# Graph and relational attention on one core: the graph projection from seven products of quarters, the last norm's statistics on ScalarE

## The chip, the cores and the metric

The kernel runs on one core of one Trainium2 chip. The metric is the device time of one execution in microseconds, median of several runs; smaller is better. A core has TensorE (PE in the profile; its weight loads are listed apart as PEld), VectorE (DVE), ScalarE (ACT), GpSimd (POOL), and SyncE (SP), which here only issues DMA transfers. Each engine works through its own queue in order; they wait for one another through semaphores.

## The reference

64 graphs of 256 nodes with 256 features pass through two layers, all in fp32.

```
def layer0(x, adj):                       # two graph attentions, then a feed-forward
    for W, a in ((W1, a1), (W2, a2)):
        Wh = h @ W
        e  = leaky_relu(Wh @ a[:F] + (Wh @ a[F:]).T, 0.2)
        h  = softmax(where(adj > 0, e, -9e15), axis=1) @ Wh
    h = norm(x + h) * g1 + b1
    return norm(h + relu(h @ wf1 + bf1) @ wf2 + bf2) * g2 + b2

def layer1(x, adj):                       # 8 heads, relations r by value of adj
    A = softmax(q k^T / sqrt(32))
    o = sum over r of (A * (adj == r)) @ v_r
    x = norm(x + o @ Wo + bo) * g1 + beta1
    return norm(x + gelu(x @ W1 + b1) @ W2 + b2) * g2 + beta2
```

`norm` subtracts the mean of a row and divides by the square root of its variance plus 1e-5.

## The kernel before

The 64 graphs are taken as 32 pairs, `g[0]` to `g[31]`. A pair is a tile of 128 partitions by four blocks of 256 features. The kernel is a pipeline of 32 turns, `turn(y_, x_, z)` with `y_ = u`, `x_ = u + 1`, `z = u + 2`: in one turn pair y_ passes through layer 1, pair x_ through layer 0's feed-forward, and pair z through layer 0's graph attentions. A prologue brings pairs 0 and 1 to that point. Thirty turns have a pair z. In them the order on TensorE, SyncE, VectorE and ScalarE is the order in which the program writes the instructions (a manual schedule); GpSimd is left to the scheduler. Where two turns meet, the scheduler may interleave the end of one with the start of the next.

What the steps of the text refer to:

- *Seven products.* Most large products are computed as a 2 by 2 block product with seven quarter products instead of eight (Strassen's scheme in Winograd's form). `Projections` (L1047) does this for queries, keys and values, `hidden_seven` (L909) for the hidden layers, with step names such as "7a" (product 7, half a), `HiddenOut` (L998) for their output layers. Sums of operand quarters are made by VectorE (`sums`, s1 to s4). Seven products share two or three PSUM banks: a later product accumulates onto the bank of an earlier one, after the earlier result has been read out (`taken` or `add`). In `HiddenOut` product 6 accumulates onto product 1, 7 onto 6, 4 onto 7, and 3 onto 5.
- *The projection* `projected` (L767) forms xp = x @ W for pair z, with four extra columns for the attention scores, so 260 columns: two matmuls and one ScalarE copy for each of four blocks. Its input xT is the transpose of x, which `early` (L1171) makes on VectorE from the tile `xq`. `load_x` (L429) fetches xq. Then `score_rows` (L778) spreads a column of xp over rows, `Softmax` (L786) has the steps `raw`, `leaky`, `exp`, `masks`, `shares` and `scaled`, and `first_sums` (L1203) multiplies the attention with xp into `hp`.
- *PSUM banks.* `bank` (L423) hands out six banks of the tag "g"; two more, "po" and "zo", hold the attention's sums. `scores(n)` takes four banks of "g" for its heads, and `exps` (L1123) on ScalarE reads them out.
- *The last norm.* The finished y of the turn before waits in `waiting`. `moments` (L860) takes its statistics by VectorE's batch-norm instructions, `norm` (L870) makes the factor rs on GpSimd, `offsets` (L883) the shift, `applied_norm` (L887) normalizes on ScalarE, `affine` (L898) multiplies by the gain and adds the bias on VectorE (`times`, `plus`), `stored` (L1242) sends it off.
- *Division.* `shares(b, parts)` of a turn turns the attention's row sums into reciprocals (part 0) and divides (part 1); `out_(b)` then runs the output projection `yop`.

Of the kernel before, what the change touches and what calls it, by code (L numbers as in the profile page):

```python
# [16 lines left out]
P = 128  # L17
# [368 lines left out]
def narrow_path(  # L386
# [93 lines left out]
    other = const.tile([P, NG], F32, name="other")  # L480

# [56 lines left out]
    def gat_weights():  # L538

        w1s = work.tile([P, KB, F], F32, tag="hT", name="gw1")  # L540
        nc.scalar.dma_start(w1s, g_W1.rearrange("(c p) f -> p c f", p=P))
        w2e = work.tile([P, KB, WX], F32, tag="wh", name="gw2e")
# [138 lines left out]
    w2s, w2m = seven_out(w2, "w2")  # L681

# [84 lines left out]
    def projected(u, hT, blocks, xp):  # L767
        if xp is None:
            xp = work.tile([P, T, WX], F32, tag="wh", name=f"xp{u}")
# [63 lines left out]
    def gat_first(u, s, xp, hp=None, blocks=range(T)):  # L833
        if hp is None:
            hp = work.tile([P, T, WX], F32, tag="wh", name=f"hp{u}")
# [34 lines left out]
    def norm(u, l, y, blocks=range(T), mv=None, rest=range(NB, T)):  # L870
# [10 lines left out]
        return blocks, mv, rs, nm  # L881

# [220 lines left out]

    isd = 1.0 / math.sqrt(DH)
# [115 lines left out]
    def out_pieces(u, y, h1):  # L1220

        if u == NG - 2:
            s = [io.tile([P, T, N], F32, tag="y", name=f"sq{u}", bufs=4),
                 work.tile([P, T, WX], F32, tag="wh", name=f"wq{u}")[:, :, :N]]
# [51 lines left out]
    def turn(y_, x_, z):  # L1276
# [49 lines left out]
        with order:  # L1326
            p.sums()
            if X:
# [15 lines left out]
            if z + 1 < NG:  # L1344
                load_x(z + 1)
            if waiting:
                w, wy = waiting[0]
                last = moments(w, 3, wy, range(NB))
            if X:
# [4 lines left out]
                moved(moves, 3)  # L1354
                times(X["y"], rg1)
# [5 lines left out]
                if waiting:  # L1361
                    last = norm(w, 3, wy, mv=last)
# [6 lines left out]
                if waiting:  # L1369
                    offsets(*last)  # L1370
# [6 lines left out]
                if waiting:  # L1377
                    applied_norm(wy, *last, [0, 1])
# [4 lines left out]
                if waiting:  # L1383
                    applied_norm(wy, *last, [2, 3])
# [4 lines left out]
                first("ra")  # L1389
                scores(3)  # L1390
# [3 lines left out]
                shares(0, [0])  # L1394
                if not y_:
# [6 lines left out]
                first("5b 4a 6b 3b")  # L1402
                masks(3, (0,))
                if Z:
                    project(z, range(0, 1))
                first("rb 7b")
                if Z:
                    project(z, range(1, 2))
                first("sb")
                masks(3, (2,))  # L1410
                totals(3)
                sums(2)
                sums(3)
                first("4b")
# [32 lines left out]
            if X:  # L1447
                out = HiddenOut(x_, 0, X["y"], X["h1"], wf2s, out_sums(x_, 0))
                if Z:
                    out.sums(1, 2)  # L1450
            if Z:
                shares(1)
# [9 lines left out]
            if Z:  # L1462
                project(z, range(T // 2, T))
            if Z:
# [7 lines left out]
            if Z:  # L1472
                first_scores(z)
# [5 lines left out]
            if Z:  # L1479
                out(1)  # L1480
# [4 lines left out]
                out.sums(4)  # L1485
# [33 lines left out]
            if waiting and Z:  # L1519
                affine(waiting[0][1], rg4, rb4)  # L1520
                stored(*waiting.pop(), slice(0, T))
            if z + 1 < NG:
                load_rows(z + 1)
# [5 lines left out]
            if Z:  # L1529
                first_sums(z, range(T // 2, T))  # L1530
            if X:
# [79 lines left out]
    waiting, late = [], []  # L1611

    with tc.manual_schedule(engines={getattr(mybir.EngineType, n) for n in
# [75 lines left out]
        load_x(2)  # L1689
# [25 lines left out]
        first_sums(1)  # L1715
        affine(a["y"], rg1, rb1)
# [20 lines left out]
        made(wvm, 4)  # L1737
        first(3)
# [73 lines left out]
```

## Time and profile before

| | |
|---|---|
| median of three runs | 2960.92 us (2951.9 to 2962.96) |
| the profiled execution's own time | 2953.9 us |
| span in its profile, first to last instruction | 2952.3 us |
| granted TensorE clock | 0.998 |
| busy: PE, DVE, ACT, POOL | 99%, 88%, 64%, 21% |
| L773, projection matmuls | 512 records, 128.0 us, mean 383 ns |
| L866 and L867, moments of all norms | 512 of 408 ns and 512 of 182 ns |
| L895, normalizing activation of 256 | 592 ns |
| L775, copy of 260 columns from PSUM | 371 ns |
| L1014, quarter sum of 128x1024 | about 1.22 to 1.28 us |

Mean durations of matmuls overlap one another, and so do those of the other engines a little; what a stream costs is read from the distance between starts. A turn takes 90 us: the same instruction returns after that time. In a row of the profile, the line number is that of the program, `out<-in` names tiles, then come the shape and the number of instructions; brackets give the idle time of the engine before it and what ended it.

### The profile page before, as it was taken

The numbers are of one execution on the slowest core, as the hardware profiler recorded it, in microseconds if no ns is written. First come the engines' busy times: TensorE is split into PE (matmuls) and PEld (weight loads), VectorE is DVE, ScalarE is ACT, GpSimd is POOL, SyncE is SP. The second block draws the span as 40 slices with busy tenths as digits, with TensorE's granted clock in tenths as the row PEclk, the third lists the DMA queues.
The fourth block names the chain that finished last, engine by engine and source line by source line (L and its number), as shares of the span: only waits on it lengthen the run. The fifth ranks groups of instructions, "written<-read, shape, count | busy, mean of one in ns | idle before, by whom it ended". The sixth has DMA issues, their size and how long they took to land.

```text
span 2952.3 us, 58648 instructions
## 1 busy us (share of the span) xinstructions
PE 2921.4 (99%) x22206; PEld 2501.8 (85%) x22206; DVE 2612.6 (88%) x5027; ACT 1898.3 (64%) x3982; POOL 629.3 (21%) x930
## 2 busy tenths in 40 slices
PE   8999999999999999999999999999999999999997
PEld 7788888888888888888888888888888888888876
DVE  5889899989989898999898998899998989988987
ACT  5566666676676666666766766766667667667652
POOL 4212221122121122221221211222212212112211
PEclk9999999999999999999999999999999999999999
DMA  5011111111111111111111111111111111111000
GB/s 152 12 31 32 38 32 34 24 40 32 37 29 23 38 32 39 32 32 24 39 32 37 31 28 31 35 37 34 30 23 40 32 37 32 29 30 33 18 8 16
DMA packets 408020, 99.27 MB, mean 34 GB/s; under 512 B 357834, under 2 KB 407220, under 8 KB 407732
## 3 DMA queue, kind: packets, MB, share of 16 engines
q1 hardware_dynamic: 406332, 94.13, 14.8%
q8 instruction: 178, 2.92, 0.4%
q0 software_dynamic: 1056, 1.05, 0.1%
q14 instruction: 110, 0.90, 0.1%
q10 hardware_dynamic: 344, 0.28, 0.0%
HBM read 56.78 MB, written 16.78 MB: 25 GB/s over the span
## 4 chain that ended last, share of the span: by engine, by line
PE 96%; DVE 2%; ACT 1%; issue 0%; POOL 0%; DMA 0%; POOLq 0%; DVEq 0%; ACTq 0%
PE yf L1028 26%; PE h1a L939 15%; PE h1b L939 11%; PE po L1144 8%; PE v L1095 6%; PE qk L1095 6%; PE sp L1116 4%; PE hpp L840 4%; PE xpp L773 4%; PE ygp L851 4%; PE yop L851 4%; PE zo L1147 2%; PE rows L782 1%; DMA first<-in_adj_dram 0%; DVE st L866 0%
## 5 line engine op out<-in xcount | busy, mean ns | idle before, releaser
L1125 ACT ACTIVATE e<-sp 128x512 f32<-128x512 f32 x512 | 270.9, 611 | 71.4 <-issue 42.8
L1129 DVE TENSOR_TENSOR ea<-e,aT 128x1024 f32<-128x1024 f32 x256 | 310.9, 1216 | 1.8 <-ACT e L1125 1.8
L895 ACT ACTIVATE y<-y,nm,rs 128x256 f32<-128x256 f32 x442 | 235.1, 592 | 63.7 <-DVE nm L885 62.9
L948 DVE TENSOR_TENSOR h<-h1a,h 128x512 f32<-128x512 f32 x293 | 197.3, 682 | 80.7 <-PE h1a L939 77.3
L951 ACT COPY h<-h1b 128x512 f32<-128x512 f32 x293 | 175.2, 599 | 124.8 <-PE h1b L939 123.2
L957 ACT ACTIVATE h<-h,cols 128x256 f32<-128x256 f32 x512 | 221.9, 502 | 36.2 <-DVE h L948 32.0
L735 POOL COPY hT<-yt 32x256 f32<-32x256 f32 x244 | 211.5, 867 | 143.3 <-DVE yt L718 128.6
L1082 ACT COPY qk<-qk 128x512 f32<-128x512 f32 x128 | 74.4, 581 | 238.9 <-PE qk L1095 238.1
L866 DVE BATCH_NORM_STATS2 st<-y 128x6 f32<-128x256 f32 x512 | 208.6, 408 | 5.6
L877 POOL TENSOR_SCALAR rs<-mv 128x4 f32<-128x4 f32 (+1 forms) x134 | 41.5, 309 | 806.8 <-DVE mv L867 445.8
L1036 DVE TENSOR_TENSOR y<-yf,y 128x256 f32<-128x256 f32 x448 | 185.5, 414 | 30.5 <-PE yf L1028 30.5
L957 ACT ACTIVATE h<-h1a,cols 128x256 f32<-128x256 f32 x256 | 102.7, 464 | 131.8 <-PE h1a L939 131.8
L1157 POOL TENSOR_TENSOR low<-low,rq 128x16 f32<-128x16 f32 x64 | 14.0, 219 | 811.9 <-DVE rq L1156 811.9
L907 DVE TENSOR_TENSOR y<-y,rb 128x1024 f32<-128x1024 f32 x126 | 163.6, 1298 | 2.2
L1134 DVE TENSOR_TENSOR es<-e 128x1024 f32<-128x1024 f32 x128 | 155.8, 1217 | 0.0
L904 DVE TENSOR_TENSOR y<-y,rg 128x1024 f32<-128x1024 f32 x126 | 153.5, 1218 | 0.1
L878 POOL TENSOR_TENSOR rs<-rs,mhalf 128x4 f32<-128x4 f32 (+1 forms) x134 | 139.9, 1044 | 8.3
L939 PE MATMUL h1a<-tt,wf 128*128 128x256 f32 x512 | 137.7, 392 | 1.5 <-DVE h L948 1.5
L1116 PE MATMUL sp<-qk 32*128 32x256 f32 x2048 | 138.3, 394 | 0.0
L1144 PE MATMUL po<-e,v 128*32 128x256 f32 x2048 | 135.5, 382 | 0.0
L1144 PE MATMUL po<-ea,v 128*32 128x256 f32 x2048 | 134.4, 379 | 0.0
L718 DVE STREAM_TRANSPOSE yt<-y 128x256 f32<-128x256 f32 x364 | 128.3, 407 | 0.8 <-ACT y L895 0.7
(285 smaller groups left out, 7733.7 us busy)
## 6 DMA issues: line engine op xcount, KB each, us to landing
hT<-yt SPq DMA_DIRECT2D x666, 32.0 KB, 1.8
y<-in_x_dram SPq DMA_DIRECT2D x32, 512.0 KB, 4.2
xq<-in_x_dram SPq DMA_DIRECT2D x240, 64.0 KB, 2.1
aq<-in_adj_dram SPq DMA_DIRECT2D x240, 64.0 KB, 2.3
out_dram<-y SPq DMA_DIRECT2D x30, 512.0 KB
wf<-in_L_gnn_w_ff_dram SPq DMA_DIRECT2D x2, 1024.0 KB, 8.6
w<-in_L_gnn_W_dram SPq DMA_DIRECT2D x2, 1024.0 KB
first<-in_adj_dram POOLq DMA_DIRECT2D x2, 512.0 KB, 9.8
```

The source lines that it names most:

```text
L735: nc.gpsimd.tensor_copy(to, at)
L851: nc.tensor.matmul(ps[:, i * F:(i + 1) * F], lhs(t, k), rhs(b, k), start=(k == 0), stop=(k == n - 1))
L866: nc.vector.bn_stats(st[:, t, :], y[:, t, :])
L895: mark["normed"] = nc.scalar.activation(y[:, t, :], y[:, t, :], AF.Identity, bias=nm[:, t:t + 1], scale=rs[:, t:t + 1])
L939: nc.tensor.matmul(ps[:, i * N:(i + 1) * N], w_[:, f * P:(f + 1) * P], m, start=first and i == 0, stop=True, skip_group_check=True)
L957: nc.scalar.activation(y, y if ps is None else ps[:, i * N:(i + 1) * N], func, bias=bi[:, f:f + 1])
L1028: nc.tensor.matmul(s.ps[n][:, i * F2:(i + 1) * F2], a[:, k, i * P:(i + 1) * P], w_[:, k, :], start=n in (1, 2, 5) and i == 0 and k == 0, s ...
L1095: nc.tensor.matmul(ps[:, i * N:(i + 1) * N], l, r, start=n in (1, 2, 5) and i == 0, stop=True, skip_group_check=True)
L1116: nc.tensor.matmul(ps[a][:, j * N:(j + 1) * N], k_[hp, m, j0:j0 + P], q[hp, m, b * N:(b + 1) * N], start=True, stop=True)
L1125: nc.scalar.activation(e[:, a, :], ps[a], AF.Exp, scale=isd)
L1129: nc.vector.tensor_tensor(ea[:, a:a + 2, :], e[:, a:a + 2, :], ab[:, None, :].to_broadcast([P, 2, NB * N]), ALU.mult)
L1144: nc.tensor.matmul(po[hp, m * N:(m + 1) * N], vs[:, hp], w[:, a, j * N:(j + 1) * N], start=(n == 0), stop=(n == len(terms) - 1))
```

## The change

1. The projection of pair z is made from seven products of quarters by a new class `Projection`, with `gwe` and three derived quarters as moving operand and quarters of xT as stationary operand. Each product is two matmuls of 130 columns. Sums of quarters of xT are made in place by VectorE, so a sum that overwrites a quarter comes after the product that reads it. ScalarE copies the results of products 2, 5, 3 and 4, VectorE adds those of 1, 6 and 7. The steps are spread through the turn, and some neighbours are moved: `out.sums(2)` later, `out.product(1)` ahead of the score rows.
2. xp takes the buffer of xq, and `hp` has one buffer. So the loads of the next xq come after `first_sums`.
3. The last norm: ScalarE sums the rows (`row_sums`) and then the squared deviations (`deviations`), GpSimd makes mean, factor and shift. The normalization runs after `first_sums`; the gain, the bias and the store run in the next turn (`done`), and the load of pair z's rows follows the store.
4. The prologue makes the derived weight quarters on GpSimd and loads x of pair 2 later.

The diff, cut to its core:

```diff
+    gwes, gwem = seven(gwe, "gwe")
...
-            xp = work.tile([P, T, WX], F32, tag="wh", name=f"xp{u}")
+            xp = io.tile([P, T, WX], F32, tag="xq", name=f"xp{u}", bufs=1)
...
+    def row_sums(sm, y, blocks):
+        for t in blocks:
+            nc.scalar.activation(y[:, t, :], y[:, t, :], AF.Identity, accum_out=sm[:, t, 0:1])
+
+    def deviations(u, sm, y):
...
+        nc.gpsimd.tensor_scalar(nm, sm[:, :, 0], -1.0 / F, 0.0, op0=ALU.mult, op1=ALU.add)
+        for t in range(T):
+            nc.scalar.activation(dump, y[:, t, :], AF.Square, bias=nm[:, t:t + 1], accum_out=sm[:, t, 1:2])
+        nc.gpsimd.tensor_scalar(rs, sm[:, :, 1], 1.0 / F, EPS, op0=ALU.mult, op1=ALU.add)
+        nc.gpsimd.tensor_tensor(rs, rs, mhalf, ALU.pow)
+        nc.gpsimd.tensor_add(high, high, sm[:, :, 0])
+        nc.gpsimd.tensor_tensor(nm, nm, rs, ALU.mult)
+        return range(T), sm, rs, nm
...
+    class Projection:
+        def __init__(s, u, hT):
+            s.u = u
+            s.xp = io.tile([P, T, WX], F32, tag="xq", name=f"xp{u}", bufs=1)
+            s.h = [[hT[k][:, b * N:(b + 1) * N] for b in range(G)] for k in range(KB)]
+
+        def sums(s, *which):
+            (h00, h01), (h10, h11) = s.h
+            for n in which:
+                o, x_, y_ = ((h00, h01, h00), (h00, h11, h00), (h01, h11, h01), (h10, h10, h00))[n]
+                nc.vector.tensor_tensor(o, x_, y_, ALU.subtract)
+
+        def product(s, n):
+            a11, a12, a22, s1, s2, s3, s4 = gwes
+            (h00, h01), (h10, h11) = s.h
+            w, m = {1: (a11, h00), 2: (a12, h10), 5: (s1, h00), 3: (s4, h11),
+                    6: (s2, h00), 7: (s3, h01), 4: (a22, h10)}[n]
+            if n == 1:
+                s.one = bank(f"xp1_{s.u}")
+            elif n == 2:
+                s.two = bank(f"xp2_{s.u}")
+            ps, c = (s.two if n in (2, 5, 3) else s.one), WX // 2
+            for i in range(NB):
+                nc.tensor.matmul(ps[:, i * c:(i + 1) * c], m[:, i * P:(i + 1) * P], w,
+                                 start=n in (1, 2, 5) and i == 0, stop=True, skip_group_check=True)
+
+        def taken(s, n):
...
+            if n in (2, 5, 3, 4):
+                nc.scalar.copy(y, ps)
+            else:
+                nc.vector.tensor_tensor(y, ps, y, ALU.add)
...
             p.sums()
+            if done:
+                times(done[0][1], rg4)
...
             p("v5")
-            if z + 1 < NG:
-                load_x(z + 1)
+            if done:
+                plus(done[0][1], rb4)
             if waiting:
                 w, wy = waiting[0]
-                last = moments(w, 3, wy, range(NB))
...
                 moved(moves, 3)
+                if waiting:
+                    row_sums(sm, wy, range(3))
+                if done:
+                    stored(*done.pop(), slice(0, T))
+                if Z and y_:
+                    load_rows(z)
                 times(X["y"], rg1)
...
-                if waiting:
-                    last = norm(w, 3, wy, mv=last)
...
                 first("ra")
+                if waiting:
+                    row_sums(sm, wy, range(3, T))
                 scores(3)
                 masks(2, (0,))
                 if Z:
                     early(z)
                 shares(0, [0])
+                if Z:
+                    xp = Projection(z, g[z]["xT"])
+                    g[z]["xp"] = xp.xp
+                    xp.product(1)
+                    xp.sums(0, 2)
...
                 first("7a sa 1b")
                 shares(0, [1])
                 masks(2, (2,))
                 totals(2)
-                first("5b 4a 6b 3b")
+                if Z:
+                    xp(2)
+                first("5b")
+                if Z:
+                    xp(5)
+                first("4a 6b 3b")
                 masks(3, (0,))
                 if Z:
-                    project(z, range(0, 1))
+                    xp(3)
                 first("rb 7b")
-                if Z:
-                    project(z, range(1, 2))
                 first("sb")
+                if waiting:
+                    last = deviations(w, sm, wy)
                 masks(3, (2,))
                 totals(3)
                 sums(2)
                 sums(3)
+                if Z:
+                    xp.taken(1)
+                    xp.sums(1, 3)
+                    xp.product(6)
                 first("4b")
...
-                    out.sums(1, 2)
...
-                shares(1)
+                out.sums(1)
+                shares(1, [0])
+                xp.taken(6)
+                shares(1, [1])
...
-                project(z, range(T // 2, T))
-            if Z:
+                xp(7)
                 early_adjacency(z)
...
             out_(1)
+                xp(4)
+                out.product(1)
                 first_scores(z)
...
-                out(1)
+                out.add(1)
                 Z["m"].scores(0)
                 Z["m"].scores(1)
                 Z["m"].exp(0)
                 Z["m"].exp(1)
-                out.sums(4)
+                out.sums(2, 4)
                 offsets(*n)
                 out(2)
...
-            if waiting and Z:
-                affine(waiting[0][1], rg4, rb4)
-                stored(*waiting.pop(), slice(0, T))
-            if z + 1 < NG:
-                load_rows(z + 1)
...
+            if z + 1 < NG:
+                load_x(z + 1)
+            if waiting:
+                applied_norm(wy, *last, range(T))
+                if Z:
+                    done.append(waiting.pop())
```

More of the change, by code (lines that the diff above doesn't have):

```diff
@@ L480, in narrow_path @@
     other = const.tile([P, NG], F32, name="other")
+    dump = const.tile([P, F], F32, name="dump")
     def weight(w, name):
@@ L541, in gat_weights @@
         nc.scalar.dma_start(w1s, g_W1.rearrange("(c p) f -> p c f", p=P))
-        w2e = work.tile([P, KB, WX], F32, tag="wh", name="gw2e")
+        w2e = work.tile([P, KB, WX], F32, tag="wh", name="gw2e", bufs=1)
         nc.sync.dma_start(w2e[:, :, :F], g_W2.rearrange("(c p) f -> p c f", p=P))
@@ L834, in gat_first @@
         if hp is None:
-            hp = work.tile([P, T, WX], F32, tag="wh", name=f"hp{u}")
+            hp = work.tile([P, T, WX], F32, tag="wh", name=f"hp{u}", bufs=1)
         for t in blocks:
@@ L881, in norm @@
         return blocks, mv, rs, nm
+    def row_sums(sm, y, blocks):
+        for t in blocks:
+            nc.scalar.activation(y[:, t, :], y[:, t, :], AF.Identity, accum_out=sm[:, t, 0:1])
+    def deviations(u, sm, y):
+        nm = work.tile([P, T], F32, tag="nm", name=f"nm{u}_3")
+        rs = work.tile([P, T], F32, tag="rs", name=f"rs{u}_3")
+        nc.gpsimd.tensor_scalar(nm, sm[:, :, 0], -1.0 / F, 0.0, op0=ALU.mult, op1=ALU.add)
[6 more added lines that the diff above has]
+        return range(T), sm, rs, nm
     def offsets(blocks, mv, rs, nm):
@@ L1102, in __call__ @@
                 s.step(n[0], int(n[1]))
+    class Projection:
[22 more added lines that the diff above has]
+        def taken(s, n):
+            b, o = {1: (0, 0), 2: (0, 0), 5: (1, 1), 6: (1, 0), 3: (1, 0), 7: (1, 1), 4: (0, 1)}[n]
+            c = WX // 2
+            y = s.xp[:, b * NB:(b + 1) * NB, o * c:(o + 1) * c]
+            ps = (s.two if n in (2, 5, 3) else s.one)[:, :WX].rearrange("p (i n) -> p i n", i=NB)
+            if n in (2, 5, 3, 4):
+                nc.scalar.copy(y, ps)
+            else:
+                nc.vector.tensor_tensor(y, ps, y, ALU.add)
+        def __call__(s, n):
+            s.product(n)
+            s.taken(n)
     isd = 1.0 / math.sqrt(DH)
@@ L1223, in out_pieces @@
             s = [io.tile([P, T, N], F32, tag="y", name=f"sq{u}", bufs=4),
-                 work.tile([P, T, WX], F32, tag="wh", name=f"wq{u}")[:, :, :N]]
+                 work.tile([P, T, WX], F32, tag="wh", name=f"wq{u}", bufs=1)[:, :, :N]]
             s += [io.tile([P, T, N], F32, tag=t, name=f"sq{u}_{t}", bufs=1) for t in ("xq", "aq")]
@@ L1343, in turn @@
             p("v5")
-            if z + 1 < NG:
-                load_x(z + 1)
+            if done:
+                plus(done[0][1], rb4)
             if waiting:
                 w, wy = waiting[0]
-                last = moments(w, 3, wy, range(NB))
+                sm = work.tile([P, T, 2], F32, tag="mv", name=f"mv{w}_3")
             if X:
@@ L1368, in turn @@
                 masks(0, (0,))
-                if waiting:
-                    offsets(*last)
                 first("1a")
@@ L1376, in turn @@
                 first("2b 3a")
-                if waiting:
-                    applied_norm(wy, *last, [0, 1])
                 masks(1, (0,))
@@ L1382, in turn @@
                 totals(1)
-                if waiting:
-                    applied_norm(wy, *last, [2, 3])
                 scores(2, ())
@@ L1462, in turn @@
             if Z:
-                project(z, range(T // 2, T))
-            if Z:
+                xp(7)
                 early_adjacency(z)
@@ L1609, in turn @@
             waiting.append((y_, y))
-    waiting, late = [], []
+    waiting, late, done = [], [], []
     with tc.manual_schedule(engines={getattr(mybir.EngineType, n) for n in
@@ L1688, in narrow_path @@
         a["hT"] = features("h1T0", ph, (nc.scalar.copy, nc.vector.tensor_copy))
-        load_x(2)
         load_rows(2)
@@ L1715, in narrow_path @@
         first_sums(1)
+        load_x(2)
         affine(a["y"], rg1, rb1)
@@ L1737, in narrow_path @@
         made(wvm, 4)
+        made(gwem, 4)
         first(3)
```

## The prediction

> **What bounds the kernel now.** I read the page first: busy shares, then the chain that ended last.
>
> ```profile
> span 2952.3 us, 58648 instructions
> ...
> PE 2921.4 (99%) x22206; PEld 2501.8 (85%) x22206; DVE 2612.6 (88%) x5027; ACT 1898.3 (64%) x3982; POOL 629.3 (21%) x930
> ...
> PE 96%; DVE 2%; ACT 1%; issue 0%; POOL 0%; DMA 0%; POOLq 0%; DVEq 0%; ACTq 0%
> ```
>
> TensorE sets the end. But a matmul that waits a little still looks busy, so I compared one steady turn with its own spacing. The turn from 1350.95 to 1440.95 us lasts 90.0 us; its groups at their undisturbed spacing sum to about 89. So nearly all of it is matmul streaming, and VectorE, at 88%, is second. The gain can only be columns taken off TensorE; the loss is any new wait on it. Spacing, from the timeline of all engines (start, duration, instruction):
>
> ```profile
> 1392.52 1.92 PE L773 MATMUL xpp<-gwe,xT 128*128 128x260 f32 x8
> ...
> 1394.28 1.89 PE L851 MATMUL yop<-wo,qk 128*128 128x256 f32 x8
> ...
> 1396.44 3.74 PE L1028 MATMUL yf<-wf,h 128*128 128x128 f32 x32
> ...
> 1400.01 3.74 PE L1028 MATMUL yf<-wf2t,eq 128*128 128x128 f32 x32
> ```
>
> One fp32 matmul shows as two records. Four projection matmuls of 260 columns take 1394.28 - 1392.52 = 1.76 us; 32 records of 128 columns take 3.57 us, 112 ns each.
>
> Where the new work begins (same view; brackets: idle time before and what ended it):
>
> ```profile
> 1375.30 1.24 DVE L1175 STREAM_TRANSPOSE xT<-xq 128x1024 f32<-128x1024 f32 x1
> ...
> 1376.30 1.15 PE L1116 MATMUL sp<-qk 32*128 32x256 f32 x16
> ...
> 1377.38 1.13 PE L939 MATMUL h1a<-tt,wf 128*128 128x256 f32 x4
> ...
> 1378.55 0.69 DVE L948 TENSOR_TENSOR h<-h1a,h 128x512 f32<-128x512 f32 x1 [1.10 <-PE h1a L939]
> ```
>
> ScalarE's first exponential of that score group, alone:
>
> ```profile
> 1377.52 0.60 ACT L1125 ACTIVATE e<-sp 128x512 f32<-128x512 f32 x1 [1.20 <-issue]
> ```
>
> And from the score rows of the next pair to the product that uses s4:
>
> ```profile
> 1396.00 0.60 PE L782 MATMUL rows<-ident,xp 128*128 128x128 f32 x4
> ...
> 1396.64 1.57 ACT L800 ACTIVATE s<-rows,xp 128x256 f32<-128x256 f32 x4 [1.79 <-PE rows L782]
> ...
> 1398.43 0.43 DVE L1036 TENSOR_TENSOR y<-yf,y 128x256 f32<-128x256 f32 x1 [0.33 <-PE yf L1028]
> ...
> 1398.77 1.28 DVE L808 SCALAR_TENSOR_TENSOR s<-s 128x512 f32<-128x512 f32 x2
> ...
> 1399.97 1.22 DVE L1014 TENSOR_TENSOR eaq<-h,eq 128x1024 f32<-128x1024 f32 x1
> ...
> 1402.20 0.42 DVE L1036 TENSOR_TENSOR y<-yf,y 128x256 f32<-128x256 f32 x1
> ...
> 1403.59 0.61 PE L1028 MATMUL yf<-wf,eaq 128*128 128x128 f32 x4
> ```
>
> The addition at 1402.20 releases the bank into which the product at 1403.59 accumulates: 1.0 us of slack today.
>
> **What the Trainium skill says.** "TensorE: Matmul & The Clock Gate", § Wait — 56ns, not 53.3ns?: a streamed matmul takes N/2.4 GHz plus about 2.5 ns. Two passes of 128 give 111.7 ns; the trace has 112. The same page, § Step-by-step, says that only weight loads are pulled ahead and matmuls stay in program order, so one that waits holds all behind it; the rows above start in program order. "PSUM — Partial Sum Buffer", § Terms: a bank must not be written by TensorE while another engine reads it. So a product into a bank not yet read out must wait; no run here could show the violation. "ScalarE: Activation LUTs", § What ACT_TABLE_LOAD costs: 186 ns + 0.833 ns per element, each pointer operand 93 more. For 256 elements with two pointers that is 585 ns; the normalization's row (L895) has 592.
>
> **The change, part by part, per turn (90 us, 30 turns with a third pair z).**
>
> *Columns.* Out: eight matmuls of 260 columns, 2 x 1.76 = 3.51 us. In: fourteen of 130, 28 records x 112 x 130/128 = 3.17 us (0.45 per product). **-0.34 us.**
>
> *ScalarE.* Four copies of 260 elements (371 ns) stay four. The normalization's four activations (2.08 us) move later. New: four row sums (skill's price 399 ns) and four squares (492), each with an accumulator read, 187 ns at L765. I take 0.6 each, bounds 0.4 and 0.8. Three row sums fall in the 1.73 us idle before the copy at 1362.38, the squares in the 4.00 us before 1391.00, the normalization in the 2.27 us before 1413.49. Cost 0. Without cover the three sums would delay the last projection copies by up to 2.4 us, and the exponentials behind them.
>
> *VectorE.* Out: four moment pairs, 2.1 us by spacing, and an offset. In: four differences of 256 (0.34 to 0.46 by spacing, 1.5 in all) and three additions from PSUM (0.34, as L1036; 1.0). The scale (1.22) runs at the turn's start, in the 1.25 us in which VectorE waits for POOL's rs; the shift takes the place of the first two moment pairs. So total work is +0.4 us, but its place counts: the 2.1 us leave a stretch before 1364.3, the 2.5 us land between 1377 and 1396, where VectorE had 1.4 us idle in 19.
>
> *POOL and SP.* POOL's three small norm operations become five, 20 us ahead of use: 0; the four weight sums in the prologue, some 3 us once, hidden between 0 and 3. On SP the store, then the load of rows into its buffer, wait for the shift and for the store's landing (2.4 us); nothing else is queued there until 1405. The eight x loads go behind the graph sums: issued in 4.8 us near 1411, ahead of the twelve moves at 1421, landing 50 us before use. 0; without that, moves late by the same 5 us would stop TensorE.
>
> *New waits on TensorE.*
> (1) Product 1 stands right after the last score group. Then all six banks of the pool are live: four of scores, two of hidden products. It must wait for the first exponential, 1377.52 + 0.60 = 1378.12, plus 0.1 for the semaphore. TensorE arrives at 1377.38: **+0.85**. In the kernel before, a product with its own bank stood here and covered this.
> (2) Product 5 takes product 2's bank after its copy, behind the delayed `sa`: **+0.1**.
> (3) VectorE goes on at 1378.87 instead of 1378.55. Until the second half of the divided outputs it has its 14.55 us, plus differences 1.5, plus additions 0.68, minus the quarter sum moved away 1.14, plus some 0.3 of waiting for matmuls: ready 1394.8. The second output product gets there at 1394.28 (0.45 of projection ahead of it, no longer 1.75): **+0.6**. Product 4 then waits for product 7's addition, behind the output addition and two moment pairs: **+0.3**.
> (4) From the rows to product 3: 0.64 until ScalarE starts, 0.95 until the first leaky step, 0.70 and 0.60 for the two, 1.26 and 1.14 for the sums 2 and 4 (2 is new here), 0.07, 0.34, 0.68 for offset, addition, masks, 0.42 for the addition that frees the bank, 0.1: 6.9 us. TensorE has 0.44 + 3 x 1.79 = 5.8 to cover it; before it had four products, 7.6, as product 1 stood behind the rows. **+1.05.**
> (5) Product 7 then waits for the difference s3: **+0.2**. The graph sums need the scaled xp at about the time at which TensorE comes: 0.
>
> Sum: -0.34 + 0.85 + 0.1 + 0.6 + 0.3 + 1.05 + 0.2 = +2.76 us; x 30 = 83 us. Upon the profiled execution's 2953.9 (span 2952.3): **3037 us**. That execution lies 7 below the median of the runs, 2960.9, within their spread (2951.9 to 2963.0). Each wait is bounded by 0 below, and by about 0.4 more than I took above.
>
> **Rivals.**
> *Only the fewer columns count:* ScalarE's exponentials come earlier, or a bank is free, and VectorE's new work fits its gaps. -0.34 x 30 = -10, at best another 0.25 per turn from gaps: 2936 to 2945. For it: VectorE waits 1.10 us at 1378.55, room for two differences, and ScalarE has room. Against: six live banks and the 5.8 to 6.9 do not hang on VectorE's load. It decides if both (1) and (4) are under 0.1. This is the rival on the other side.
> *Only part of the waits:* (4) alone gives (1.05 - 0.34) x 30 = +21, 2975; (1) and (4) give +47, 3001. For it: (3) and (5) rest on VectorE's spacing, summed over 16 us.
> *ScalarE binds too:* row sums at 0.8 and late normalization delay the hidden copies at 1413 by up to 1 us: 3067. Against: 64% busy.
>
> **How the numbers follow.** All waits 0.50 (3014 to 3060), part 0.24 (2970 to 3014), columns only 0.20 (2936 to 2965), more 0.06. A difference under 0.5%, 15 us, is about what cannot be told from no change. Columns only mostly falls inside that: faster 0.08, same 0.15, slower 0.77. Range 2948 to 3062: it leaves out most of the faster cases and the worst, some 0.15. The likeliest case's own is 3014 to 3060.
>
> **What would show it.** Projection groups of 130 columns spaced 0.45 us; the first of them 0.8 us after the scores, ended by ScalarE's exponential; a gap before the second `yop` group and before the s4 product; the turn at 92 to 93 us; VectorE idle 0.7 before the leaky step. A turn of 89.7 us would prove me wrong, and a first product right after the scores would refute (1).

## The result

The changed kernel took 3063.62 us in the median of six runs (3056.64 to 3067.74), the kernel before 2961.72 (2951.9 to 2963.05, six runs): a ratio of 1.0351, 95% interval 1.0335 to 1.0366. The prediction had the direction and most of the mechanism. Its point was 3037 us in a range of 2948 to 3062 us; the time lies 27 us above the point and 1.6 us beyond the upper end of the range. In the profiles of this case the first turn begins either about 90 us or about 98 us after the first instruction (89.8 us in the changed kernel, 97.8 us in a variant with the same source up to there), so single times can differ by 8 us for that reason alone, and gains are read below from the length of a turn.

### The profile page after: what moved, and what is told of

It is laid out like the page before. It is cut to its first block, busy times and chain, and to the rows that moved or that the text cites. A ratio compares the mean times of both kernels' runs of the same rounds, so it can differ in the third digit from the quotient of the medians.

```text
span 3054.9 us, 60089 instructions
## 1 busy us (share of the span) xinstructions
PE 2965.5 (97%) x22566; PEld 2503.9 (82%) x22566; DVE 2620.1 (86%) x4967; ACT 2011.9 (66%) x4462; POOL 607.5 (20%) x994
## 3 DMA queue, kind: packets, MB, share of 16 engines
q0 software_dynamic: 1056, 1.05, 0.2%
## 4 chain that ended last, share of the span: by engine, by line
PE 48%; DVE 29%; ACT 14%; issue 4%; POOL 3%; DMA 1%; DVEq 0%; ACTq 0%; SPq 0%; POOLq 0%
PE yf L1047 9%; PE h1b L958 8%; PE h1a L958 7%; PE po L1206 6%; DVE eq L1033 4%; ACT h L976 4%; PE hpp L842 4%; DVE y L923 3%; PE sp L1178 3%; PE v L1114 3%; PE xp L1149 3%; DVE eaq L1033 3%; PE qk L1114 2%; DVE st L868 2%; DVE y L1055 2%
## 5 line engine op out<-in xcount | busy, mean ns | idle before, releaser
L737 POOL COPY hT<-yt 32x256 f32<-32x256 f32 x244 | 176.1, 722 | 133.7 <-PE qk L1114 81.4
L879 POOL TENSOR_SCALAR rs<-mv 128x4 f32<-128x4 f32 (+1 forms) x104 | 26.2, 252 | 720.7 <-DVE mv L869 495.0
L868 DVE BATCH_NORM_STATS2 st<-y 128x6 f32<-128x256 f32 x392 | 161.0, 412 | 4.6
L923 DVE TENSOR_TENSOR y<-y,rg 128x1024 f32<-128x1024 f32 x126 | 160.0, 1270 | 0.1
L1047 PEld LDWEIGHTS yf<-wf,eaq 128*128 128x128 f32 x1024 | 119.1, 192 | 38.2 <-DVE y L1055 25.6
L1047 PE MATMUL yf<-wf,eaq 128*128 128x128 f32 x1024 | 130.9, 282 | 20.0 <-DVE y L1055 19.7
L1158 ACT COPY xp<-xp 128x260 f32<-128x260 f32 x120 | 44.4, 370 | 153.4 <-PE xp L1149 153.4
L976 ACT ACTIVATE h<-h1a,cols 128x256 f32<-128x256 f32 x256 | 102.6, 464 | 61.3 <-PE h1a L958 61.3
```

What stands on the lines that cost most here:

```text
L868: nc.vector.bn_stats(st[:, t, :], y[:, t, :])
L923: nc.vector.tensor_mul(y, y, g_[:, None, :].to_broadcast(list(y.shape)))
L976: nc.scalar.activation(y, y if ps is None else ps[:, i * N:(i + 1) * N], func, bias=bi[:, f:f + 1])
L1047: nc.tensor.matmul(s.ps[n][:, i * F2:(i + 1) * F2], a[:, k, i * P:(i + 1) * P], w_[:, k, :], start=n in (1, 2, 5) and i == 0 and k == 0, s ...
```

## The profile after

The page of the changed kernel, its profiled execution at 3056.64 us:

```profile
span 3054.9 us, 60089 instructions
...
PE 2965.5 (97%) x22566; PEld 2503.9 (82%) x22566; DVE 2620.1 (86%) x4967; ACT 2011.9 (66%) x4462; POOL 607.5 (20%) x994
...
PE 48%; DVE 29%; ACT 14%; issue 4%; POOL 3%; DMA 1%; DVEq 0%; ACTq 0%; SPq 0%; POOLq 0%
```

The shares of busy time hardly moved. The chain did: TensorE's part of it fell from 96% to 48%, and VectorE and ScalarE now release what TensorE waits for. TensorE is "busy" 44 us more, although it has fewer columns to stream, because a matmul that waits a little is drawn longer; so I count by distances between starts. A turn, taken at the first query product of two turns, is 93.42 us long, before 89.97. The 3.45 us, times 30 turns, are 103 us, and 101.9 were measured. In the two traces, 102.2 of the 102.6 us by which the span grew lie between the first query products of the first and of the thirty-first turn: the loss lies in the turns, not in the prologue.

Two sets of products meet in what follows: products 1, 2, 5, 3, 6, 7 and 4 of the projection (tile `xp`) and those of the feed-forward's output (tile `yf`). Products 1, 2, 4 and 5 are the projection's, and products 3, 6 and 7 the feed-forward's where nothing else is said.

TensorE in one turn of after, which starts at 1306.30 (timeline: start, duration, engine, line, operation; in brackets idle time and what ended it):

```profile
1314.43 1.13 PE L1114 MATMUL qk<-tq,wqk 128*128 128x256 f32 x4 [0.20 <-ACT qk L1101]
...
1332.29 1.15 PE L1178 MATMUL sp<-qk 32*128 32x256 f32 x16
1334.15 0.71 PE L1149 MATMUL xp<-gwe,xT 128*128 128x130 f32 x4 [0.71 <-ACT e L1187]
...
1336.43 0.61 PE L1149 MATMUL xp<-gwe,xT 128*128 128x130 f32 x4
1336.87 1.03 PE L958 MATMUL h1b<-tt,wf1s 128*128 128x256 f32 x4
...
1350.67 1.99 PE L853 MATMUL yop<-wo,qk 128*128 128x256 f32 x8 [0.21 <-DVE qk L1226]
1352.79 0.71 PE L1149 MATMUL xp<-gwe,xT 128*128 128x130 f32 x4
...
1357.35 4.01 PE L1047 MATMUL yf<-wf2t,eq 128*128 128x128 f32 x32
1361.99 2.05 PE L1047 MATMUL yf<-wf,eaq 128*128 128x128 f32 x16 [0.64 <-DVE y L1055]
```

A quarter product of the projection costs 0.44 to 0.45 (1336.43 to 1336.87), as forecast; over all turns it is 0.446, so that seven take 3.12 where the eight matmuls of 260 columns took 3.51: -0.39. The first one comes 1.86 us after the score group ahead of it, which itself needs 1.08: 0.78 of waiting for the first exponential. `yop` is 0.37 late (0.82 after the product ahead of it instead of 0.45), and takes 2.12 to the next start where it took 1.73 before, and product 4 takes 0.55 instead of 0.44: 0.50 more. The 32 records at 1357.35, products 5 and 6 of the feed-forward, need 3.58, and product 3 starts after 4.64: 1.06, of it 0.17 ahead of product 6 and the rest ahead of product 3. Around product 7, later in the trace, the distances are 1.89, 1.91 and 1.89 instead of 1.79, 1.74 and 1.79: 0.37. Ahead of product 7 itself the trace names the cause. Its weight load (PEld) waits for the quarter sum s3, which ends 0.05 before it:

```profile
1364.38 1.36 DVE L1033 TENSOR_TENSOR eaq<-h 128x1024 f32<-128x1024 f32 x1
...
1365.79 1.86 PEld L1047 LDWEIGHTS yf<-wf,eaq 128*128 128x128 f32 x16 [0.41 <-DVE eaq L1033]
```

All of these stand where the prediction put them. The first row of the turn does not: the product of quarters q7, at 8.13 us into the turn, waits for ScalarE's copy of q6. In the kernel before it starts 7.77 us into its turn, which begins at 1350.95, and without idle time:

```profile
1358.72 1.03 PE L1095 MATMUL qk<-tq,wqk 128*128 128x256 f32 x4
```

By the first score group 0.64 us are lost (12.82 us into the turn, before 12.18): 0.36 ahead of q7, 0.17 and 0.11 behind it. That loss is not in the prediction. I call it wait (0).

VectorE in the same trace, where the turn before ends:

```profile
1304.77 0.40 DVE L868 BATCH_NORM_STATS2 st<-y 128x6 f32<-128x256 f32 x1
1305.08 1.21 DVE L923 TENSOR_TENSOR y<-y,rg 128x1024 f32<-128x1024 f32 x1
1306.20 0.18 DVE L869 BATCH_NORM_AGGREGATE mv<-st 128x2 f32<-128x6 f32 x1
1306.29 0.66 DVE L856 TENSOR_TENSOR y<-ygp,y 128x512 f32<-128x512 f32 x1
...
1309.72 0.16 DVE L904 SCALAR_TENSOR_TENSOR nm<-mv,rs 128x4 f32<-128x4 f32 x1 [1.25 <-POOL rs L880]
```

And the same place in the kernel before, whose turn starts at 1350.95:

```profile
1350.20 0.66 DVE L854 TENSOR_TENSOR y<-ygp,y 128x512 f32<-128x512 f32 x1
...
1353.62 0.16 DVE L885 SCALAR_TENSOR_TENSOR nm<-mv,rs 128x4 f32<-128x4 f32 x1 [1.25 <-POOL rs L878]
```

The scale (L923), written at the start of the turn, behind its first sums, has run in the middle of the statistics that end the turn before. The output addition behind it starts at -0.01 us of the turn instead of -0.75, and the offsets at 3.42 instead of 2.67. The 1.25 us of idle time, in which the prediction put the scale, is still there. What hangs on the offsets is about as late: ScalarE's normalization, and behind it in ScalarE's queue the copies of q5, q6 and v6. The normalization and the copy of q6, after:

```profile
1309.92 2.08 ACT L914 ACTIVATE y<-y,nm,rs 128x256 f32<-128x256 f32 x4 [1.05 <-DVE nm L904]
...
1313.79 0.58 ACT L1101 COPY qk<-qk 128x512 f32<-128x512 f32 x1
```

And before:

```profile
1353.81 2.08 ACT L895 ACTIVATE y<-y,nm,rs 128x256 f32<-128x256 f32 x4 [0.29 <-DVE nm L885]
...
1357.77 0.59 ACT L1082 COPY qk<-qk 128x512 f32<-128x512 f32 x1
```

They start 3.62 and 7.49 us into the turn instead of 2.86 and 6.82.

VectorE between the score rows of the next pair and product 3, after:

```profile
1356.69 1.42 DVE L810 SCALAR_TENSOR_TENSOR s<-s 128x512 f32<-128x512 f32 x2 [0.72 <-ACT s L802]
1358.03 1.22 DVE L1033 TENSOR_TENSOR eq<-eq,h 128x1024 f32<-128x1024 f32 x1
1359.28 1.22 DVE L1033 TENSOR_TENSOR eaq<-h,eq 128x1024 f32<-128x1024 f32 x1
...
1361.52 0.42 DVE L1055 TENSOR_TENSOR y<-yf,y 128x256 f32<-128x256 f32 x1
```

Quarter sum 2 (1358.03) now stands between the leaky step and sum 4, with 0.72 us of idle time ahead of the leaky step, and the addition that frees product 3's bank ends at 1361.94, 0.05 before the product.

## The experiments

All of these kernels compute the whole reference. My theory was the list of waits with (0) added; the rival, that VectorE or ScalarE has simply too much to do, in which case a wait that is taken away comes back further on. A time without an interval is one execution, and its 8 us at the start can hide a gain; the length of the turn does not contain them.

### The scale behind the last addition of the turn

```diff
             p.sums()
-            if done:
-                times(done[0][1], rg4)
...
             out(4)
+            if done:
+                times(done[0][1], rg4)
             waiting.append((y_, y))
```

> The gain of the last norm (times(done), 1.22 us of VectorE) is written behind the last addition of a turn instead of behind p.sums() of the next one. Theory W (single waits, each with its place): it fills VectorE's 1.25 us wait for rs, the offsets come 0.75 us earlier, TensorE no longer waits for the copies of qk and v: the turn shrinks from 93.4 to 92.8 us, the profiled time from 3057 to about 3038. Rival A (ScalarE is late because of its new row sums): no change, 93.4.

Measured: turn 93.24, 3062.04 us. Forecast 92.8: missed, a gain of 0.18 only. The scale did go where it was meant to, behind the statistics. VectorE there:

```profile
1406.71 1.22 DVE L923 TENSOR_TENSOR y<-y,rg 128x1024 f32<-128x1024 f32 x1
1408.85 0.16 DVE L904 SCALAR_TENSOR_TENSOR nm<-mv,rs 128x4 f32<-128x4 f32 x1 [0.92 <-POOL rs L880]
```

GpSimd in the same run, the power that makes rs:

```profile
1406.96 1.85 POOL L880 TENSOR_TENSOR rs<-rs,mhalf 128x4 f32<-128x4 f32 x1
```

The same power takes 1.04 us in the kernel before and in after; beside the scale it takes 1.85, and ends 0.88 after the scale's end. So the idle time was not free: what VectorE runs in it puts off what it is waiting for, and 0.46 of the 0.64 us stay. The Trainium skill describes such a case ("SBUF — State Buffer", § Who interferes with whom): an instruction of VectorE with two inputs in SBUF contends with a GpSimd instruction that reads SBUF, for a read interface that only one of them holds at a time. The times agree with it: the power begins 0.25 after the scale, and 0.88 of it is left when the scale is over, though spans on GpSimd are rough. 29 powers of this run take 1.85, none in after.

### Product 1 behind step 7a

```diff
-                    xp.product(1)
-                    xp.sums(0, 2)
...
-                first("7a sa 1b")
+                first("7a")
+                if Z:
+                    xp.product(1)
+                    xp.sums(0, 2)
+                first("sa 1b")
```

> Product 1 of the projection stands behind hidden product 7a instead of right behind the last scores, with its two differences. Theory W: it no longer waits for the first exponential to free a bank (0.71 us of wait on record), and VectorE goes on about 0.7 us earlier, so that the wait of the second output product shrinks too: turn 92.3 to 92.7 us, about 3022 to 3036 us. Rival V (VectorE has too much work between 1332 and 1356, wherever it starts): the wait comes back at the second output product and product 4, turn 93.1 or more.

Measured: turn 92.55, 3040.55 us. The wait for the bank is gone and the turn is 0.87 shorter, its 0.78 and the 0.08 of product 5. A product that has its bank now covers the exponential. The waits at `yop` and behind it stayed as they were, although the forecast had that at `yop` shrinking.

### Sum 2 ahead of the leaky step

```diff
                 out.add(1)
+                out.sums(2)
                 Z["m"].scores(0)
...
-                out.sums(2, 4)
+                out.sums(4)
```

> The quarter sum s2 of the first feed-forward stands ahead of the leaky step, where VectorE waits 0.72 us for ScalarE, instead of behind it. Theory W: the chain from the score rows to product 3 loses 1.26 and gains about 0.45, and the wait ahead of product 3 (with that ahead of product 6 1.06 us) falls to 0.2 to 0.4: turn 92.6 to 92.8 us, about 3033 to 3039. Rival V: no gain, 93.3 or more, the graph sums wait instead.

Measured: turn 92.35, 3034.63 us, a gain of 1.06, more than the 0.6 to 0.8 that I gave it. TensorE there:

```profile
1351.72 3.74 PE L1047 MATMUL yf<-wf2t,eq 128*128 128x128 f32 x32
1355.31 2.05 PE L1047 MATMUL yf<-wf,eaq 128*128 128x128 f32 x16
```

3.59 us from one to the other instead of 4.64: the whole wait ahead of products 6 and 3 is gone. Sum 2 fits the idle time ahead of the leaky step, and a wait that I had put down to a chain of 6.9 us was an order in it.

### These three together

> The three moves together. Theory W: the waits are separate, so their gains add, -0.64 - 0.9 - 0.7: turn 91.1 to 91.4 us, time 2985 to 2997. Rival V: VectorE's work binds, the turn stays above 92.2, over 3020. If moving removed all waits the turn would be 89.7.

Measured: 2999.98 us (2995.58 to 3005.66), ratio 1.0149, interval 1.0124 to 1.0174; turn 91.30. The gains add: 0.18 + 0.87 + 1.06 = 2.11, and 93.42 - 91.30 = 2.12. The turn is as forecast, the time 3 us above the forecast's upper end. None of the waits had hidden another one.

### Each half of the change alone

The norm's half alone keeps parts 2 and 3 of the change, and takes the eight products back to their places:

```diff
-                    xp.product(1)
-                    xp.sums(0, 2)
...
-                first("4a 6b 3b")
+                first("5b 4a 6b 3b")
...
+                    project(z, range(0, 1))
...
+                    out.sums(1, 2)
...
-                xp(7)
+                project(z, range(T // 2, T))
...
-                out.sums(2, 4)
+                out.sums(4)
```

The projection's half alone takes the last norm back:

```diff
-                times(done[0][1], rg4)
...
-                plus(done[0][1], rb4)
...
-                sm = work.tile([P, T, 2], F32, tag="mv", name=f"mv{w}_3")
+                last = moments(w, 3, wy, range(NB))
...
-                    row_sums(sm, wy, range(3))
...
-                    last = deviations(w, sm, wy)
...
+                affine(waiting[0][1], rg4, rb4)
```

> Only the last norm's part of the change (statistics on ScalarE, scale and shift a turn later, loads and buffers as changed); the projection again from eight products, with the quarter sums and the first output product where they were before. Theory W: the four waits around the projection are gone, only that at the turn's start stays, turn 90.5 to 90.7 us, time 2972 to 2983. Rival A (ScalarE's extra work holds others): 91 or more, over 2990. If the norm's part cost nothing: 90.0, as before.

> Only the projection from seven products, with its loads, buffers and moved neighbours; the last norm as before (moments on VectorE, scale and shift in the middle of the turn). Theory W: the wait at the turn's start is gone, those at the bank, at the second output product and product 4, and at the s4 product stay or grow by the moments on VectorE, turn 92.7 to 93.2 us, 3035 to 3052. Rival: without VectorE's relief the turn is far longer than with it, 94 or more; that would say that the norm's part paid for itself.

Measured, norm alone: 2974.98 us (2971.42 to 2979.18), ratio 1.0054, interval 1.0035 to 1.0074; turn 90.60, and the only wait in it is (0), at 8.12 us into the turn. Projection alone: turn 92.76, 3049.81 us; q7 at 7.77 as before, and the waits for the bank (0.71 in brackets), at `yop` (0.21) and at product 3 (0.64) all as in after. Over the turn before they cost 0.63 and 2.79, together 3.42 of the 3.45. So wait (0) belongs to the norm alone, (1) to (5) to the projection alone, and neither half pays for the other. ScalarE's new sums cost nothing here: the norm's half has no loss beyond the 0.63 up to the first scores.

### Scale and shift together behind v5

```diff
             p.sums()
-            if done:
-                times(done[0][1], rg4)
...
             p("v5")
             if done:
-                plus(done[0][1], rb4)
+                affine(done[0][1], rg4, rb4)
```

> The gain of the last norm stands right ahead of its bias, behind the transposes and v5, and so neither ahead of the last statistics nor beside GpSimd's power for rs (which took 1.85 us instead of 1.04 in the run before with the gain beside it). Theory P (the gain is in the way of the norm's offsets, by its place): TensorE's wait of 0.64 us for the copies of qk and v goes, turn 92.7 to 92.9 us, about 3035 to 3042 us. Rival A (the row sums on ScalarE): still 93.2 to 93.4.

> Product 1 behind 7a, s2 ahead of the leaky step, gain and bias together behind v5. Theory W: against the three moves before (91.3 us with the gain at the turn's end) another 0.46 go, turn 90.8 to 90.9 us, 2979 to 2985; what is left is 0.76 at the second output product and product 4 and 0.36 at the graph sums, less the 0.34 of fewer columns. Rival V: VectorE's new work only moves the wait, 91.2 or more.

Measured, alone: turn 93.31, 3061.74 us; with the other moves: 3003.57 us (2998.27 to 3005.29), ratio 1.0150, interval 1.0131 to 1.0169, turn 91.36. Both forecasts missed. In the run alone q7 starts at 7.78 again, but the wait has moved three products on:

```profile
1323.56 1.13 PE L1114 MATMUL qk<-tq,wqk 128*128 128x256 f32 x4 [0.25 <-DVE qk L1098]
```

The two pieces, 2.5 us, now stand together ahead of VectorE's additions for the queries and values (L1098), and q4 is 0.42 late for them, the first scores 0.53. Here the rival of the second forecast holds (91.2 or more): the work only moves the wait. The number of the first one's rival, 93.2 to 93.4 with ScalarE's row sums as the cause, fits too; but q7 is on time with these sums in place, and the next run takes the rest away with them in place as well.

### The scale behind v5, the shift behind the first hidden step

```diff
-                plus(done[0][1], rb4)
+                times(done[0][1], rg4)
...
-                if done:
-                    stored(*done.pop(), slice(0, T))
-                if Z and y_:
-                    load_rows(z)
...
                 steps = first_hidden(x_)
+                if done:
+                    plus(done[0][1], rb4)
+                    stored(*done.pop(), slice(0, T))
+                if Z and y_:
+                    load_rows(z)
```

> The changed kernel with two pieces of the last norm moved: the scale (VectorE, 1.21 us) goes to where the shift stood, behind the copy of v5, and the shift with its store and the load of the next rows goes on past the first hidden step of the feed-forward. The scale alone then takes the 1.2 us that the shift took at that place, so the copy of q4 should not be late as it was with scale and shift together (10.78 us into the turn), and the offsets' steps start early enough for q6 and v6. Theory: wait (0) is gone and none comes in its place; the turn falls by 0.5 to 0.7 us from 93.42 to about 92.8, the time to about 3040 us. Rival: the 1.2 us of the shift are now late somewhere else on VectorE (the copies behind the first hidden step); then the turn stays at 93.2 or more.

Measured: turn 92.77, 3046.16 us: a gain of 0.65, the whole of wait (0), and q7, v7, q4 and the first scores stand at 7.77, 8.64, 10.36 and 12.18 us into the turn, as in the kernel before. A store and a load that start later cost nothing. The turn is that of the projection alone, 92.76: with the scale and the shift at these places the norm's half costs nothing. Wait (0) was one of place, not of VectorE's load.

### All moves, with the first sums of x ahead of 7a

To the last run, product 1 behind 7a and sum 2 ahead of the leaky step, this adds:

```diff
+    apart = const.tile([P, N], F32, name="apart")
...
-                o, x_, y_ = ((h00, h01, h00), (h00, h11, h00), (h01, h11, h01), (h10, h10, h00))[n]
+                o, x_, y_ = ((apart, h01, h00), (apart, h11, apart), (h01, h11, h01), (h10, h10, apart))[n]
...
-            w, m = {1: (a11, h00), 2: (a12, h10), 5: (s1, h00), 3: (s4, h11),
-                    6: (s2, h00), 7: (s3, h01), 4: (a22, h10)}[n]
+            w, m = {1: (a11, h00), 2: (a12, h10), 5: (s1, apart), 3: (s4, h11),
+                    6: (s2, apart), 7: (s3, h01), 4: (a22, h10)}[n]
```

so that sums 0 and 2 need not wait for product 1 and stay ahead of 7a.

> All of the waits that I found are taken on together: the scale and the shift as in the run with the shift later; the second sum of the output ahead of the leaky scores (as in the third run); product 1 of the projection behind step 7a; and the first difference of x in a tile of its own, so that its sums need not wait for the last read of the old one and run in VectorE's idle time of 1.1 us ahead of 7a, which would let the waits of the second output product (0.37) and of product 4 (0.39) go. Theory: each wait goes without a new one, and the turn is 91.36 (the four moves) less 0.53 (q4), 0.76 (output product and product 4) and up to 0.36 (around product 7), so 89.7 to 90.1 us, the time 2950 to 2965 us: level with the kernel before. Rival: VectorE has no idle time left ahead of these places (its load of 86% binds there), the waits of product 4 and of the output product stay, and the turn is 90.8 us or more, the time over 2985 us.

Measured: 2981.78 us (2980.86 to 2983.57), ratio 1.0084, interval 1.0067 to 1.0102; turn 90.83. The three gains add again (93.42 - 0.65 - 0.87 - 1.06 = 90.84), and the tile apart brought nothing: the rival's turn, though not its time of over 2985. In this trace VectorE is idle for only 0.12 us between 1395.97 and 1423.6, and the rest of the loss lies in that stretch: 0.37 at `yop`, 0.50 behind it, 0.37 around product 7. The next two runs ask whether order or load makes them.

### Only the order in that stretch

```diff
-                out.sums(1)
                 shares(1, [0])
                 xp.taken(6)
                 shares(1, [1])
+                out.sums(1)
...
+                xp(7)
                 mv = moments(y_, 2, y, range(NB))
...
-                xp(7)
                 early_adjacency(z)
```

> The last kernel with two pieces of VectorE's order in the output stage changed and nothing added or removed: the mask product of the feed-forward (1.22 us) goes behind the second normalised attention output, on which the second output product waits, and product 7 is taken up ahead of the norm's statistics, so that product 4 finds its tile free. In its trace VectorE has no idle time from 16 us before to the end of product 3 (1395.97 to 1425.0), so the two ideas of what the waits are part here. If each wait is due to the order alone, the waits of the output product (0.37) and of product 4 (0.39) go and the turn is 90.83 less 0.76, about 90.1. If VectorE's whole load in this stretch is what binds, both waits go from where they were and come back around product 7 and the second graph sums, and the turn stays at 90.7 to 90.9. I expect the second.

Measured: turn 90.72, 2978.55 us. `yop` and product 4 now start without a wait, and TensorE stands again ahead of product 3:

```profile
1418.13 2.05 PE L1048 MATMUL yf<-wf,eaq 128*128 128x128 f32 x16 [0.59 <-DVE y L1056]
```

The two waits were worth 0.87 here (0.37 and 0.50); 0.75 are lost at product 3, which starts 4.33 us after the 32 records ahead of it instead of 3.58. Product 3 starts 53.02 us into the turn, and 53.13 us into it in the run before: the same work of VectorE stands ahead of it, in another order. Here VectorE's load binds, and a better order only moves the wait. (The stretch without idle time that the forecast names ends at 1423.66 in that trace, not at 1425.0; product 3 lies within both.)

### Less work in that stretch, in the old order

```diff
+            s.free = s.xp[:, :NB, WX // 2:WX // 2 + P]
...
-                o, x_, y_ = ((apart, h01, h00), (apart, h11, apart), (h01, h11, h01), (h10, h10, apart))[n]
+                o, x_, y_ = ((apart, h01, h00), (s.free, h11, apart), (h01, h11, h01), (h10, h10, s.free))[n]
...
-                    6: (s2, apart), 7: (s3, h01), 4: (a22, h10)}[n]
+                    6: (s2, s.free), 7: (s3, h01), 4: (a22, h10)}[n]
...
-                    xp.sums(0, 2)
+                    xp.sums(0, 1, 2)
...
                 if Z:
-                    xp.product(1)
+                    xp(2)
+                    xp.sums(3)
                 first("sa 1b")
...
-                    xp(2)
+                    xp.product(1)
                 first("5b")
...
-                    xp.sums(1, 3)
```

> The last kernel of all waits, in VectorE's old order, but with the other two sums of the projection (0.83 us) out of the dense stretch: product 2 comes ahead of product 1, the sum for product 6 is written into a quarter of the result that nothing uses before product 4, and so three sums stand ahead of step 7a, where VectorE was idle for 0.37 us, and the fourth behind it, where it was idle for 0.62. Theory that VectorE's load in the output stage binds: everything in the stretch comes 0.83 us earlier, the output product's wait (0.37), that of product 4 (0.39) and most of the gaps around product 7 (0.36) go, the turn is 89.7 to 90.1 us and the time 2949 to 2960 us, level with the kernel before or just below it. Rival: the place of the sums makes no difference, or the first step of 7a's sum is late in their place and holds TensorE there; the turn is then 90.6 or more, the time 2975 us or more.

Measured: 2974.45 us (2968.15 to 2977.26), ratio 1.0053, interval 1.0038 to 1.0067; turn 90.37. The sums went into the idle time; what is left of it ahead of the hidden addition, and idle time that is new, ahead of the output addition:

```profile
1398.40 0.69 DVE L968 TENSOR_TENSOR h<-h1a,h 128x512 f32<-128x512 f32 x1 [0.29 <-PE h1a L959]
...
1411.75 0.69 DVE L857 TENSOR_TENSOR y<-yop,y 128x512 f32<-128x512 f32 x1 [0.23 <-PE yop L854]
```

The gain is 0.46, between the two forecasts. `yop` no longer waits (0.37 gained), behind it 0.40 of the 0.50 stay, and the 0.37 around product 7 stay. Together with the run above: up to product 3 VectorE's load bound in the run of all moves, and product 3 now starts 52.66 us into the turn instead of 53.13. The rest is not load alone. VectorE is now idle for 0.23 us until `yop` is there, and only then come the output addition, two moment pairs and the addition of the projection's product 7, for which product 4 waits: what is left behind `yop` is an order, the one that the run above changed. With both edits some more may go; that was not tried. The balance over the kernel before closes: -0.39 for the columns, +0.40, +0.37: 0.38, measured 0.40. This is the fastest form of the seven products that I found, and it is slower than the eight.

## Why the prediction was wrong, point by point

Per turn, in us (30 turns):

| Step of the prediction | forecast | measured in after | settled by |
|---|---|---|---|
| columns | -0.34 | -0.39 (0.45 a product, as forecast) | spacing alone |
| (1) product 1 waits for the exponential | +0.85 | +0.78 | gone with product 1 behind 7a |
| (2) product 5 | +0.1 | +0.08 | the same run |
| (3) `yop`, product 4 | +0.6, +0.3 | +0.37, +0.50 | order alone moves them to product 3; less work takes 0.47 of them |
| (4) from the rows to product 3 | +1.05 | +1.06 | gone with sum 2 ahead of the leaky step |
| (5) around product 7 | +0.2 | +0.37 | the trace alone: 0.17 ahead of product 7, which waits for s3; no run removes it |
| the scale in VectorE's idle time | 0 | +0.64 | norm alone; gone with the scale moved |
| ScalarE, POOL, SP, prologue | 0 | 0 | norm alone; the turns give the whole loss |
| sum | +2.76 | +3.45 (the rows give 3.41) | |

*The step that failed* is the sentence "The scale (1.22) runs at the turn's start, in the 1.25 us in which VectorE waits for POOL's rs", costed at nothing. It is worth 0.64 a turn, 19 us in all. Upon the forecast that gives 2953.9 + 30 x 3.40 = 3056, and the profiled execution took 3056.64. So 19 of the 27 us between the point and the median are this step. The other 7 are the execution on which the sum was put: it lies some 7 us below its kernel's median, as 3056.64 lies 7 us below 3063.62. Two things were wrong in that sentence. Where two turns meet, the order written is not the order run, as the description of the kernel says: the scale went into the end of the turn before, ahead of the very statistics that rs waits for. And the idle time would not have hidden it at its own place either: with the scale in it the power on GpSimd took 1.85 us instead of 1.04, and only 0.18 of the 0.64 came back. The prediction did say of other covers what they cost if they are gone; for this one it did not ask.

*Right, with numbers.* (1), (2) and (4) are within 0.07. The wait of (1) is ended by the exponential in the trace (0.71 in brackets), and is gone in the run that puts a product with a bank of its own in between. Of the signs that the prediction named, the 0.45 a product, the 0.8 ahead of the first one and VectorE's 0.7 ahead of the leaky step all came; the turn, 93.42, lies above its 92 to 93. In (4) the size was right, and its reason as well, sum 2 in the chain; that this was an order and could be undone at no cost was not seen.

*Right in sum only.* For (3) and (5) I took 1.1 and 1.24 was measured, with too much at `yop` and too little behind it and around product 7. Since these waits move into one another (0.87 gone and 0.75 back in the run of order alone), one number for all of it would have been the better forecast.

*The rivals.* "Only the fewer columns count" is refuted by its own test: (1) and (4) are 0.78 and 1.06, not under 0.1. "Only part of the waits" is refuted too, since every wait of the list is in the trace. "ScalarE binds too" named a cause that does not show here: the turn is 92.77 with ScalarE's sums and the late normalization (the run with the shift later) and 92.76 without them. That its number, 3067, is near the result is chance.

## What to carry to other kernels

Before an instruction goes into an engine's idle time, ask what ends that time, and whether the instruction holds up just that: an engine that waits for a small step of another is not free if its work slows that step, as the scale slowed the power from 1.04 to 1.85 us. Place it by the trace and not by the source where a scheduler may interleave. And when fewer columns are bought with more operations on the second-busiest engine, sum that engine's work over the stretch where it lands: here 0.39 us of columns were bought with sums and additions that leave 0.77 us of waits in the best form found.

## What the hardware showed that I had not expected

- The power of 128x4 elements on GpSimd went from 1.04 to 1.85 us beside one VectorE multiplication of 1.22 us. In the run with sum 2 ahead of the leaky step, another power of 128x4 took 1.92 us beside that sum; there nothing waited for it. So the contention named above shows in an operation of four elements per partition too.
- The idle time that the profile shows in brackets on TensorE is only part of a wait: ahead of product 3 it is 0.64, and 1.06 came back when the cause was removed; ahead of q7 it is 0.20, and q7 starts 0.36 late. At product 3 another 0.27 is drawn as longer matmuls (4.01 instead of 3.74 for the same 32 records), and undisturbed records are drawn 0.16 into the next group (3.74 for a distance of 3.58).
- The costs of separate waits added to within 0.03 us up to the run of all moves. From there on VectorE's idle time in the output stage was used up, and they no longer did: two waits worth 0.87 us went in the run of order alone, and the turn became 0.11 us shorter.
